# Norm statistics of the last workspace layer, queued pair by pair behind the masked steps of the layer before it

## The chip, the cores and the metric

The kernel runs on one core of a Trainium2 chip. The metric is the device time of one execution in microseconds, lower is better. The engines are TensorE (PE in the profile, with its weight loads as PEld), VectorE (DVE), ScalarE (ACT), GpSimd (POOL) and SyncE (SP), which issues the DMAs. Each engine works through a queue of its own in order, and waits on semaphores for the others.

## The reference

A stack of eight residual layers on an input of 4 sequences x 512 positions x 256 features, all float32. The last two matter here: the low-rank attention layer and the second pass of the workspace layer. Every layer normalizes its input first.

```python
def _layernorm(x, axis=-1, eps=1e-05):
    m = jnp.mean(x, axis=axis, keepdims=True)
    v = jnp.var(x, axis=axis, keepdims=True)
    return (x - m) / jnp.sqrt(v + eps)
...
    # _L1_attn_b_ref, the low-rank layer: 16 heads of 16, causal
    Q = _multilora(x, ids, Wq, Aq, Bq)
    ...
    scores = jnp.einsum('bhqd,bhkd->bhqk', Q, K) / jnp.sqrt(jnp.asarray(D_KV, x.dtype))
    causal = jnp.tril(jnp.ones((s, s), bool))
    scores = jnp.where(causal, scores, jnp.asarray(-jnp.inf, scores.dtype))
    attn = jax.nn.softmax(scores, axis=-1)
    out = jnp.einsum('bhqk,bhkd->bhqd', attn, V)
    out = out.transpose(0, 2, 1, 3).reshape(b, s, D_MODEL)
    return _multilora(out, ids, Wo, Ao, Bo)
...
    x = x + _L1_ffn_ref(_layernorm(x, axis=-1), ...)      # workspace layer, first pass
    x = x + _L1_attn_b_ref(_layernorm(x, axis=-1), ...)   # low-rank layer
    x = x + _L1_ffn_ref(_layernorm(x, axis=-1), ...)      # workspace layer, second pass
    return x
```

## The kernel before

The residual stream stays on the chip: `self.x[b]` holds sequence b as 128 partitions x 4 tiles x 256 features. A *tile* below is one of these [128, 256] pieces, numbered i. The layers run one after another. TensorE's queue is in program order; the queues of VectorE, ScalarE and GpSimd are set by a scheduler with its own estimates of time.

**The low-rank layer** (`lora_stage`, method `run`) goes through 16 units `todo`, 4 sequences x 4 groups of 4 heads. Its loop over n works on three units at once, in a pipeline. Round n has four steps m = 0 to 3:

- `maxima` of unit n + 1: TensorE makes scores (L1507) into two PSUM buffers. VectorE runs four *masked steps* on them (L256, `masked`): each adds the causal mask, and its running minimum, fetched by an accumulator read, is a row maximum with its sign turned. Step m works on 512, 384, 256 and 128 keys. Each pair of masked steps frees a PSUM buffer.
- `weights` of unit n: TensorE makes scores again (L1507), ScalarE takes the exponential (L1539, `lo_ex`), and GpSimd zeroes the upper triangle (L1540, a select).
- at m = 0, `values` of unit n - 1 (L1550 on TensorE, 32 matmuls; then ScalarE's copy to `lo_og`, L1555); at m = 1, `divided` (transposes L1563, then L1566 and L1567 on VectorE).
- at m = 3 after a sequence's last group, `output` part 0 (L1578, L1580); at m = 0 of the round after, part 1: 16 matmuls (L238) and the addition to `x` (L1591). With that the sequence's `x` is final for this layer.
- after m = 3, `lowered`: transposes (L1528) and `lo_qm` (L1530).

In some rounds `prepare` also works on the next sequence: `adapted` (matmuls L238 from `s4b`, then `lo_wvob`, L1446), `project` (matmuls L238, then L1469 on VectorE, L1473 on ScalarE, `lo_wide` L1475 and L1476 on GpSimd), `turn` (L1482, L1486). All PSUM tiles of this stage come from one tag with four buffers, used in turn:

```python
with m.psum("ps_3", two=4), pool("lora_2", 2) as l2:
    run(l2)
```

**The workspace layer** (`ws`) starts with `enter(b)` for the four sequences. `layernorm` calls `moments`: on VectorE four `bn_stats` (L178), one for each tile, and four `bn_aggr` (L179) that make mean and variance. Then the inverse root of the variance for all four tiles at once: `rpow` takes one step on VectorE (L154), Ln and Exp on ScalarE (L155, L156), and three more steps on VectorE (L157, L158, L160); L195 makes an offset. `rpow_aside` is the same with the small steps on GpSimd (L141, L144 to L147, and L192, L193 for the offset), Ln and Exp on L142 and L143; before, it serves the first pass for b = 0 and 1, and an earlier layer twice. ScalarE then writes the normalized `ws_xf` (L203).

For b = 0, 1, 2 of the second pass, the input is final long before `ws` begins, and the scheduler had put their statistics into the low-rank layer's loop: right behind the addition to `x` (L1591), in rounds n = 5, 9 and 13, among the masked steps of m = 1. The statistics of the fourth sequence have to wait for the last addition.

Of the kernel before, what the change touches and what calls it, by code (L numbers as in the profile page):

```python
# [16 lines left out]
P = 128  # L17
# [8 lines left out]
class Model:  # L26
# [142 lines left out]

        self.tc.keep_in_program_order(self.nc.scalar.preload_act_table_set("natural_log_exp_and_others"))  # L170

    def moments(self, src, aside=False):

        nc = self.nc
        st = self.small.tile([P, NI, 6], F32, name="ln_st", tag="ln_st")
        mv = self.small.tile([P, NI, 2], F32, name="ln_mv", tag="ln_mv")
        for i in range(NI):
            nc.vector.bn_stats(out=st[:, i, :], in_=src[:, i, :])  # L178
            nc.vector.bn_aggr(out=mv[:, i, :], in_=st[:, i, :])  # L179
        rstd = self.small.tile([P, NI], F32, name="ln_rstd", tag="ln_rstd")  # L180
        (self.rpow_aside if aside else self.rpow)(rstd, mv[:, :, 1], 1.0, 1e-5, self.tmps())
        return mv, rstd

    def layernorm(self, dst, src, by_scalar=False, aside=False):

        nc = self.nc
        mv, rstd = self.moments(src, aside)
        if by_scalar:
            both = by_scalar == "both"
            off = self.small.tile([P, NI], F32, name="ln_off", tag="ln_off")  # L190
            if aside:
                nc.gpsimd.tensor_tensor(off, mv[:, :, 0], rstd, op=ALU.mult)  # L192
                nc.gpsimd.tensor_scalar_mul(off, off, -1.0)  # L193
            else:
                nc.vector.scalar_tensor_tensor(off, mv[:, :, 0], -1.0, rstd, op0=ALU.mult, op1=ALU.mult)  # L195
            for i in range(NI):
                if both and i % 2:
                    nc.vector.tensor_scalar(
                        dst[:, i, :], src[:, i, :], mv[:, i, 0:1], rstd[:, i : i + 1],
                        op0=ALU.subtract, op1=ALU.mult,  # L200
                    )
                    continue
                nc.scalar.activation(  # L203
                    dst[:, i, :], src[:, i, :], AF.Identity, bias=off[:, i : i + 1], scale=rstd[:, i : i + 1]
                )
            return mv, rstd
        for i in range(NI):
            nc.vector.tensor_scalar(
                dst[:, i, :], src[:, i, :], mv[:, i, 0:1], rstd[:, i : i + 1],
                op0=ALU.subtract, op1=ALU.mult,  # L210
            )
# [41 lines left out]

    def masked(self, sc, n, nmax):

        self.nc.vector.tensor_tensor_reduce(  # L256
            out=sc[:, :n], in0=sc[:, :n], in1=self.mask[:, T - n :], scale=-1.0, scalar=3.0e38,
            op0=ALU.add, op1=ALU.min, accum_out=nmax,
        )
# [760 lines left out]
    def ws_fold(self, w, pool, once):  # L1020
# [47 lines left out]
        for h in range(4):  # L1068
            m, rows = h % 2, slice(h * 32, h * 32 + 32)
            nc.vector.tensor_tensor(w["ob"][rows], w["ob"][rows], pb[rows, m, :D], op=ALU.add)  # L1070
    def ws(self, w, order, woven={}):

        nc, S, R = self.nc, 16, P
        with self.pool("ws_1", 1) as p1, self.pool("ws_2", 2) as p2:
# [258 lines left out]

            if True:
                def enter(b):
                    mv, rstd = self.layernorm(xf[b], self.x[b], "both" if b == B - 1 else True, bool(woven) and b < 2)
                    nc.vector.tensor_tensor(ms[:, :, b], mv[:, :, 1], rstd, op=ALU.mult)
                    nc.vector.tensor_tensor(ms[:, :, b], ms[:, :, b], rstd, op=ALU.mult)
                    turned(b, int(b == 2))

                for b in range(B):
                    if b == B - 1:
                        with self.tc.high_priority(offset=2000):
                            enter(b)
                    else:
                        enter(b)
                flat = ms.rearrange("p i b -> p (i b)")
                self.rpow(
                    flat, flat, 1.0, 1e-6, [tile([P, NI * B], f"rp{k}") for k in range(2)],
                    norm.rearrange("p i (b s) -> p (i b) s", s=32),  # L1350
                )
                for rnd in range(2):
                    st = written(gathered(picked(rnd == 0)), rnd)
                    wqk, cst = folded(st)
                    vo = None
                    for n in range(B + 5):
                        if n < B:
                            attend(n, wqk, cst)
                        if n == 1:
                            vo = outputs(st)  # L1360
                        if 0 <= n - 3 < B and rnd == 0:
                            carried(n - 3)
                        if 0 <= n - 2 < B:
                            turn(n - 2)
                        if 0 <= n - 3 < B:
                            read(n - 3, vo, rnd)
                        if 0 <= n - 5 < B and rnd == 0:
                            turned(n - 5, 2 * (n > 6), True)
                        if (rnd, n) in woven:
                            next(woven[rnd, n], None)  # L1370
# [5 lines left out]
    def lora_load(self, wp, shared):  # L1376
        nc = self.nc
        st = wp.tile([P, 4], I32, name="lo_st", tag="lo_st")
        nc.sync.dma_start(out=st, in_=self.a["lo_starts"].partition_broadcast(P))
        w = {n: self.load(shared[0], f"lo_{n}") for n in ("wqk", "wvo")}  # L1380
        w |= {n: self.load(shared[1], f"lo_{n}") for n in ("aqk", "avo", "bqk")}
        w |= {n: self.load(shared[2], f"lo_{n}") for n in ("bvo", "lidx")}
        w["cos"], w["sin"] = self.load(wp, "rope16_c"), self.load(wp, "rope16_s")

        stf = wp.tile([P, 4], F32, name="lo_stf", tag="lo_stf")
        nc.vector.tensor_copy(stf, st)
        cnt = wp.tile([P, B], F32, name="lo_cnt", tag="lo_cnt")
        for b in range(B):
            le = wp.tile([P, 4], F32, name=f"lo_le{b}", tag=f"lo_le{b}")
            nc.vector.tensor_scalar(le, stf, float(b), None, op0=ALU.is_le)  # L1390
            nc.vector.tensor_reduce(cnt[:, b : b + 1], le, axis=AX.X, op=ALU.add)
        nc.gpsimd.tensor_scalar(cnt, cnt, 1.0, 0.0, op0=ALU.subtract, op1=ALU.max)
        w["lm"] = lm = wp.tile([P, B], F32, name="lo_lm", tag="lo_lm")
        nc.vector.tensor_scalar(lm, cnt, 3.0, w["lidx"], op0=ALU.min, op1=ALU.is_equal)
        return w
# [22 lines left out]
    def lora_stage(self, w, order, tiles, wpool):  # L1418
# [93 lines left out]
        def maxima(s, g, m):  # L1512

            i = NI - 1 - m
            n = (i + 1) * P
            nm = nmt[g % 2]
            scs = scored(n, slice(i * P, n), s.qk[:, 0, g, :], s.qk[:, 1, g, :n])
            with self.tc.high_priority(offset=500):
                for pair, sc in enumerate(scs):
                    for k in range(2):  # L1520
                        at = (pair * 2 + k) * 32 + ONE
                        self.masked(sc[:, k, :], n, nm[:, i, at : at + 1])

        def lowered(s, g):

# [83 lines left out]
        def run(pool):  # L1609
# [7 lines left out]
                maxima(*todo[0], m)  # L1617
            seqs[1].wqk = adapted(seqs[1], "qk")
            lowered(*todo[0])
            at = (2, 5, 6, 7, 8, 9, 10)  # L1620
            for n in range(len(todo) + 2):
                s, g = todo[n] if n < len(todo) else (None, None)
                nxt = todo[n + 1] if n + 1 < len(todo) else None
                prev = todo[n - 1] if 0 < n <= len(todo) else None
                last = todo[n - 2] if n > 1 else None
                for m in range(NI):
                    if nxt:
                        maxima(*nxt, m)
                    if prev and m == 0:
                        values(*prev)  # L1630
                    if s:
                        weights(s, g, m)
                        if s is not seqs[-1] and g * NI + m in at:
                            prepare(seqs[seqs.index(s) + 1], at.index(g * NI + m))
                    if prev and m == 1:
                        divided(*prev)
                    if prev and prev[1] == G - 1 and m == 3:
                        output(prev[0], 0)
                    if last and last[1] == G - 1 and m == 0:
                        output(last[0], 1)  # L1640
                if nxt:
                    lowered(*nxt)

        return first, run

# [7 lines left out]
def emit(tc, aps):  # L1653


    with ExitStack() as ctx:
# [49 lines left out]
        with pool("lora_1", side="right") as l1, pool("lora_w", 2) as lw, m.norms("norm_2", xn=1, xt=2):  # L1706
# [2 lines left out]
                g = first()  # L1709
                m.ws(ws, ("by", "xt", "xf"), {(1, n): g for n in (1, 2, 4, 8)})  # L1710
            with m.psum("ps_3", two=4), pool("lora_2", 2) as l2:
                run(l2)
        with m.psum("ps_4", two=2, acc=4):
            m.ws(ws, ("xf", "xt", "by"))
        m.store()


# [119 lines left out]
```

## Time and profile before

| what | value |
|---|---|
| median of 3 runs | 2172.09 us (2165.91 to 2174.39) |
| the profiled execution, its own time | 2169.45 us |
| its span, first to last instruction | 2167.7 us |
| mean granted TensorE clock | 0.969 |
| busy: PE, DVE, ACT, POOL | 92%, 59%, 35%, 27% |
| `bn_stats` (L178) in the loop | 12, mean 412 ns |
| `bn_aggr` (L179) in the loop | 12, mean 162 ns |

The profile is of one execution. "Busy" is the share of the span in which an engine ran; TensorE's includes the time in which it runs at half clock. The granted clock is a share of full speed. In timelines, the bracket behind an instruction gives how long its engine had been idle before it, and whose work ended that.

### The profile page before, as it was taken

To read this page: it belongs to the slowest core of one execution; us is meant where nothing else is said; L and a number is where in the kernel's file an instruction comes from. 1 tells how busy PE (TensorE), PEld (TensorE's weight loads), DVE (VectorE), ACT (ScalarE), POOL (GpSimd) and SP (SyncE) were. 2 spreads that over 40 slices of the span, in tenths; PEclk is the share of its full clock that TensorE was granted. 3 is DMA by queue.
4 is the path that set the end of the run, shared out by engine and by line. 5 is a ranking of instruction groups with operands and counts; after the bars stand their busy time and mean duration, and the time that the engine had idled before them with its cause. 6 is when DMAs were issued, how large, how long until landed. Compare 5 with 4: busy or idle time off the path is not lost.

```text
span 2167.7 us, 25625 instructions
## 1 busy us (share of the span) xinstructions
PE 1994.9 (92%) x9414; PEld 1066.2 (49%) x9414; DVE 1271.4 (59%) x3185; ACT 760.9 (35%) x1696; POOL 577.3 (27%) x530
## 2 busy tenths in 40 slices
PE   7999999999899999999999999987888989899886
PEld 4556555564544554544454554533355644444464
DVE  5565655756447435644754355498855766657445
ACT  2433434434323222322232233243224324334442
POOL 2433333433312112211312122175620122212100
PEclk9999999999999999999999999999799999999898
DMA  5020000000000000000000000010000000000001
GB/s 176 1 90 1 1 1 1 1 1 1 21 0 0 1 0 0 0 1 0 0 1 0 1 0 1 19 27 0 1 25 1 1 1 1 1 1 1 1 1 40
DMA packets 19837, 22.87 MB, mean 11 GB/s; under 512 B 4832, under 2 KB 17664, under 8 KB 19328
## 3 DMA queue, kind: packets, MB, share of 16 engines
q1 hardware_dynamic: 19712, 21.24, 3.0%
q8 instruction: 74, 1.21, 0.2%
q14 instruction: 51, 0.42, 0.1%
HBM read 19.14 MB, written 2.10 MB: 10 GB/s over the span
## 4 chain that ended last, share of the span: by engine, by line
PE 63%; DVE 16%; issue 11%; ACT 5%; POOL 3%; DMA 1%; SPq 0%; POOLq 0%; DVEq 0%; ACTq 0%
PE ps_two L238 26%; PE ps_acc L238 11%; PE ps_two L390 5%; PE ps_acc L429 3%; PE ps_two L1507 3%; DVE ps_two L256 3%; PE ps_two L417 2%; POOL e L687 2%; PE ps_two L1550 2%; DVE gs L888 1%; PE ps_acc L1248 1%; DVE ln_st L178 1%; PE ps_two L654 1%; ACT prob L397 1%; PE ps_st L884 1%
## 5 line engine op out<-in xcount | busy, mean ns | idle before, releaser
L687 POOL TENSOR_TENSOR e<-e 128x1024 f32<-128x1024 f32 x64 | 150.7, 2355 | 619.4 <-ACT e L679 592.2
L256 DVE CUSTOM_DVE_ANT_0 ps_two<-ps_two,mask 128x256 f32<-128x256 f32 (+3 forms) x512 | 249.6, 503 | 71.8 <-PE ps_two L390 40.8
L679 ACT ACTIVATE e<-ps_two 128x1024 f32<-128x1024 f32 x128 | 130.7, 1023 | 346.9 <-PE ps_two L238 346.7
L238 PE MATMUL ps_acc<-e,cv 128*128 128x512 f32 x512 | 234.9, 601 | 1.4 <-DVE cot L685 0.9
L402 POOL TENSOR_TENSOR prob<-prob,psum_row 128x256 f32<-128x256 f32 (+3 forms) x128 | 159.6, 1255 | 283.0 <-DVE psum_row L401 276.8
L238 PE MATMUL ps_two<-cq,ckt 128*128 128x512 f32 x512 | 230.5, 593 | 3.0 <-DVE cq L656 3.0
L397 ACT ACTIVATE prob<-ps_two,nmax 128x128 f32<-128x128 f32 (+3 forms) x256 | 132.5, 525 | 147.0 <-DVE nmax L256 137.8
L238 PEld LDWEIGHTS ps_acc<-e,cv 128*128 128x128 f32 x512 | 93.5, 190 | 138.4 <-issue 116.5
L238 PEld LDWEIGHTS ps_two<-cq,ckt 128*128 128x128 f32 x512 | 96.6, 190 | 116.9 <-issue 114.5
L238 PE MATMUL ps_two<-own_xt,s 128*128 128x512 f32 x200 | 109.6, 680 | 18.8 <-DVE prt L129 10.6
L238 PE MATMUL ps_two<-own_xt,s16a 128*128 128x512 f32 x256 | 114.9, 592 | 0.1
L238 PE MATMUL ps_two<-s16b,cot 128*128 128x256 f32 x512 | 113.1, 379 | 0.0
L1539 ACT ACTIVATE lo_ex<-ps_two 128x1024 f32<-128x1024 f32 (+3 forms) x128 | 85.2, 704 | 69.7 <-PE ps_two L1507 65.3
L390 PE MATMUL ps_two<-kvt,qx 64*128 64x256 f32 (+3 forms) x512 | 103.6, 481 | 6.1 <-ACT qx L378 2.4
L238 PEld LDWEIGHTS ps_two<-s16b,cot 128*128 128x128 f32 x512 | 97.3, 190 | 20.1 <-issue 7.7
L417 PEld LDWEIGHTS ps_two<-ident,prob 128*128 128x128 f32 x640 | 71.0, 142 | 73.4 <-issue 48.2
L417 PE MATMUL ps_two<-ident,prob 128*128 128x128 f32 x640 | 94.6, 279 | 12.9 <-ACT qx L378 4.5
L1540 POOL TENSOR_SCALAR_AFFINE_SELECT lo_ex<-lo_ex 128x256 f32<-128x256 f32 x128 | 51.7, 408 | 188.8 <-ACT lo_ex L1539 187.7
L688 DVE TENSOR_TENSOR es<-e 128x512 f32<-128x512 f32 x64 | 43.9, 686 | 95.0 <-POOL e L687 93.9
L390 PE MATMUL ps_two<-kpe,qy 64*128 64x256 f32 (+3 forms) x512 | 90.7, 431 | 0.9 <-POOL qy L324 0.9
L1507 PE MATMUL ps_two<-lo_qm,lo_t 32*128 32x128 f32 (+3 forms) x512 | 75.1, 473 | 11.1 <-ACT lo_ex L1539 4.7
L429 PE MATMUL ps_acc<-prt,kv 128*64 128x256 f32 (+3 forms) x512 | 78.8, 451 | 2.7 <-DVE prt L129 2.7
(429 smaller groups left out, 3412.6 us busy)
## 6 DMA issues: line engine op xcount, KB each, us to landing
x<-in_x SPq DMA_DIRECT2D x4, 512.0 KB, 7.5
s16b<-in_mla_wo SPq DMA_DIRECT2D x1, 2048.0 KB, 18.4
s16a<-in_cos_wq SPq DMA_DIRECT2D x1, 2048.0 KB, 8.8
s16b<-in_cos_wo SPq DMA_DIRECT2D x1, 2048.0 KB, 8.2
out_x<-x SPq DMA_DIRECT2D x4, 512.0 KB, 2.9
s16a<-in_mla_wqn SPq DMA_DIRECT2D x1, 1536.0 KB, 12.3
s<-in_mla_wqa SPq DMA_DIRECT2D x1, 1024.0 KB, 9.3
s4a<-in_mla_wkb SPq DMA_DIRECT2D x1, 512.0 KB, 6.8
```

Source lines behind the costliest of these rows:

```text
L238: self.nc.tensor.matmul(out, lhsT=l, rhs=r, start=k == 0, stop=k == n - 1)
L256: self.nc.vector.tensor_tensor_reduce(out=sc[:, :n], in0=sc[:, :n], in1=self.mask[:, T - n :], scale=-1.0, scalar=3.0e38, op0=ALU.add, op1 ...
L390: nc.tensor.matmul(sc[:, k, :n], lhsT=q[r, rows], rhs=key[r, :n], start=first, stop=not first)
L397: nc.scalar.activation(pr[:, k, :n], sc[:, k, :n], AF.Exp, bias=nm[:, k : k + 1], scale=-1.0, accum_out=sm[:, k : k + 1],)
L402: nc.gpsimd.tensor_tensor(pr[:, :, :n], pr[:, :, :n], sm.unsqueeze(2).to_broadcast([P, 2, n]), op=ALU.mult)
L417: nc.tensor.transpose(pt[:, k, keys], pr[:, k, keys], self.ident)
L429: nc.tensor.matmul(po[k * R : (k + 1) * R, j * P :], lhsT=s.kv[:, j, 0, :], rhs=prt[:, k, j, j * P :], start=j == 0, stop=j == NI - 1,)
L679: nc.scalar.activation(t.e[:, pair * 2 : pair * 2 + 2, :], sc, AF.Exp)
L687: nc.gpsimd.tensor_tensor(e2, t.e[:, 0:2, :], t.e[:, 2:4, :], op=ALU.add)
L1507: nc.tensor.matmul(scs[k // 2][:, k % 2, : keys], lhsT=left[r, rows], rhs=right[r], start=True, stop=True)
L1539: nc.scalar.activation(ex[:, hs, :], sc[:, :, :n], AF.Exp, scale=0.25)
L1540: nc.gpsimd.affine_select(out=ex[:, hs, :P], in_=ex[:, hs, :P], compare_op=ALU.is_ge, fill=0.0, base=0, pattern=[[0, 2], [1, P]], channel_ ...
```

## The change

`maxima` returns its last masked step, and `run` collects these (`ends`) and hands the second `ws` three lists of four: for each of sequences 0 to 2, the ends of m = 1, 2, 3 in the round that finishes its `x`, and of m = 0 in the next. `moments` then queues one pair of `bn_stats` and `bn_aggr` behind each of them on VectorE. The results lie in a tile of their own for each sequence (`lo_stat`) instead of rotating small buffers, and the small steps take the `rpow_aside` form, on GpSimd. In the changed kernel, the GpSimd offset steps are L198 and L199, and the statistics L185 and L186. The order behind a masked step is a place in the queue: it adds no semaphore wait.

On the queues this moves 12 `bn_stats` and 12 `bn_aggr`, takes 15 small steps off VectorE and puts 21 on GpSimd. On ScalarE the three Ln and three Exp move: for sequences 0 and 1, Ln stands ahead of the next copy to `lo_og` and Exp behind it; for sequence 2, both stand ahead of it.

```diff
-    def moments(self, src, aside=False):
+    def moments(self, src, aside=False, after=None):
...
-        st = self.small.tile([P, NI, 6], F32, name="ln_st", tag="ln_st")
-        mv = self.small.tile([P, NI, 2], F32, name="ln_mv", tag="ln_mv")
+        if after:
+            place, ends = after
+            st, mv, rstd = place[:, :, 0:6], place[:, :, 6:8], place[:, :, 8]
+        else:
...
         for i in range(NI):
-            nc.vector.bn_stats(out=st[:, i, :], in_=src[:, i, :])
-            nc.vector.bn_aggr(out=mv[:, i, :], in_=st[:, i, :])
-        rstd = self.small.tile([P, NI], F32, name="ln_rstd", tag="ln_rstd")
+            with self.tc.issue_after(ends[i].ins) if after else ExitStack():
+                nc.vector.bn_stats(out=st[:, i, :], in_=src[:, i, :])
+                nc.vector.bn_aggr(out=mv[:, i, :], in_=st[:, i, :])
         (self.rpow_aside if aside else self.rpow)(rstd, mv[:, :, 1], 1.0, 1e-5, self.tmps())
...
-                    mv, rstd = self.layernorm(xf[b], self.x[b], "both" if b == B - 1 else True, bool(woven) and b < 2)
+                    mv, rstd = self.layernorm(
+                        xf[b], self.x[b], "both" if b == B - 1 else True, b < (2 if woven else len(after)),
+                        after[b] if b < len(after) else None,
+                    )
...
+        w["stat"] = [wp.tile([P, NI, 10], F32, name=f"lo_stat{b}", tag=f"lo_stat{b}") for b in range(B - 1)]
...
                     if nxt:
-                        maxima(*nxt, m)
+                        ends.append(maxima(*nxt, m))
...
+            return [(w["stat"][n], ends[(n * G + G + 1) * NI + 1 :][:NI]) for n in range(B - 1)]
...
-                run(l2)
+                after = run(l2)
         with m.psum("ps_4", two=2, acc=4):
-            m.ws(ws, ("xf", "xt", "by"))
+            m.ws(ws, ("xf", "xt", "by"), after=after)
```

## The prediction

> **What bounds the kernel now.** I read the page first: its chain of waits says that TensorE carries the time, with VectorE behind it.
>
> ```profile
> PE 63%; DVE 16%; issue 11%; ACT 5%; POOL 3%; DMA 1%; SPq 0%; POOLq 0%; DVEq 0%; ACTq 0%
> PE ps_two L238 26%; PE ps_acc L238 11%; PE ps_two L390 5%; PE ps_acc L429 3%; PE ps_two L1507 3%; DVE ps_two L256 3%; PE ps_two L417 2%; POOL e L687 2%; PE ps_two L1550 2%; DVE gs L888 1%; PE ps_acc L1248 1%; DVE ln_st L178 1%; PE ps_two L654 1%; ACT prob L397 1%; PE ps_st L884 1%
> ```
>
> Then I asked where the twelve moved `bn_stats` (L178) run: four each at 1845.5, 1923.4 and 1999.5 us, all in the loop of the low-rank layer (about 1763 to 2038 us). I call these places batches 1, 2, 3. The timeline of batch 3 (start us, us, engine, line, in brackets the idle time before and who ended it):
>
> ```profile
> 1999.54 1.40 DVE L178 BATCH_NORM_STATS2 ln_st<-x 128x6 f32<-128x256 f32 x4
> ...
> 2001.52 0.42 PEld L1563 LDWEIGHTS ps_two<-ident,lo_og 128*128 128x128 f32 x4 [2.02 <-DVE ln_mv L179]
> ...
> 2002.75 0.21 ACT L155 ACTIVATE ln_rstd<-rp 128x4 f32<-128x4 f32 x1 [2.46 <-DVE rp L154]
> ```
>
> The four `bn_stats` stand between the first and second masked step of a group of four. Those masked steps free the PSUM buffer that TensorE needs, so TensorE sits 2.02 us. ScalarE sits 2.46 us at L155, which is queued ahead of the second exponential. In batch 1 a third wait follows:
>
> ```profile
> 1849.78 0.36 DVE L157 TENSOR_TENSOR rp<-rp,ln_rstd 128x4 f32<-128x4 f32 x1 [1.06 <-ACT ln_rstd L156]
> ...
> 1850.65 1.21 DVE L1446 TENSOR_TENSOR lo_wvob<-s,ps_two 128x1024 f32<-128x1024 f32 x1
> ...
> 1851.91 0.30 PEld L1507 LDWEIGHTS ps_two<-lo_qm,lo_t 32*128 32x128 f32 x4 [1.74 <-DVE lo_wvob L1446]
> ```
>
> VectorE waits for ScalarE before a 4-element step; behind it queues `lo_wvob`, for which TensorE waits 1.74 us.
>
> Last, an ordinary round without statistics (12.6 us long):
>
> ```profile
> 1822.90 0.59 ACT L1555 COPY lo_og<-ps_two 128x512 f32<-128x512 f32 x1 [4.11 <-PE ps_two L1550]
> 1823.42 0.14 DVE L256 DVE_READ_ACCUMULATOR2_ANT lo_nm<- 128x1 f32 x1
> 1823.62 0.31 PEld L1507 LDWEIGHTS ps_two<-lo_t 32*128 32x128 f32 x8 [0.55 <-DVE lo_nm L256]
> ...
> 1824.58 0.57 DVE L256 CUSTOM_DVE_ANT_0 ps_two<-ps_two,mask 128x384 f32<-128x384 f32 x1 [1.02 <-PE ps_two L1507]
> ...
> 1825.01 0.30 PEld L1507 LDWEIGHTS ps_two<-lo_qm,lo_t 32*128 32x128 f32 x4 [1.08 <-ACT lo_ex L1539]
> ```
>
> VectorE has gaps at fixed places: 1.02 us after the masked steps of m = 0, 0.43 before L1566, 0.75 before L1530. The copy of `lo_og` and the exponentials after it release TensorE.
>
> **The change, part by part.** On TensorE and SyncE the order of instructions stays; on ScalarE only six small steps move; on VectorE only the statistics and fifteen small steps. No DMA moves. New positions per batch: one `bn_stats` and `bn_aggr` pair behind the four masked steps of m = 1, 2, 3 of the same round, and of m = 0 of the next. Then seven small steps on GpSimd, with Ln and Exp on ScalarE.
>
> *Removed at m = 1.* The four masked steps take 2.46 us back to back (1824.58 to 1827.04). In batch 1 the first starts at 1845.05, so all end at 1847.51. One new pair follows: 0.41 for `bn_stats` plus 0.15 for `bn_aggr`, 0.55 together, to 1848.06. `lo_wvob` then waits only for TensorE's four matmuls (1.98 us, now from 1846.4), and starts at 1848.45 instead of 1850.65: 2.2 us earlier. Batch 2 the same way: masked steps from 1922.94, matmuls 1924.27 to 1926.25, `lo_wvob` at 1926.35 instead of 1927.78, 1.45 us. Batch 3 has no `lo_wvob`: masked steps 1999.06 to 2001.52, pair to 2002.07, L1566 and L1567, and m = 2 starts at 2002.7 instead of 2004.45. That is 1.75 us, and L195 (0.16) goes too: 1.9.
>
> *The other pairs.* At m = 2 in batches 1 and 2 VectorE idles afterwards (2.10 and 4.15 us before L1469): nothing. In batch 3 the steps of m = 3 follow without a gap: 0.5 lost. At m = 3 the gap is 2.76 us before L1469 (batch 1) or 0.75 before L1530 (ordinary rounds): nothing. At m = 0 of the next round it is 3.84 us or 1.02: nothing. Without this cover each pair would cost 0.55.
>
> *The small steps.* GpSimd's rows from the first use of this layer: 0.20 us each, 0.29 from start to start (L147, L192, L193), some 2.5 us a batch with the wait for ScalarE. Behind them GpSimd queues the selects of the next exponentials, whose readers come a round later, and `lo_wide`, needed more than 3 us later: nothing. The results are needed at 2038.7 us (`ws_xf`).
>
> *The added wait.* The new Ln (L142) stands on ScalarE ahead of the copy of `lo_og`, and waits for GpSimd (L141), which waits for the last `bn_aggr`. In batch 3 the Exp stands there too. By the ordinary round: the last accumulator read starts at 1823.42, `bn_stats` to 1823.83, `bn_aggr` to 1824.03, L141 to 1824.3, Ln and Exp to 1824.75. So `lo_og` is copied about 1.8 us late and the first exponential runs about 1.2 us late; TensorE's weights wait for exactly that ([1.08 <-ACT lo_ex L1539]). In batches 1 and 2 sixteen matmuls and transposes (1868.0 to 1871.7) lie before the next use of these buffers: hidden, with 1 us over. Batch 3 has none: I take 1.1 us. Bounds: 0.7 if that round starts at half clock, as it does in the trace (masked steps and L1550 then end together), and 1.8 if the whole delay of the copy counts.
>
> *Sum.* 2.2 + 1.45 + 1.9 - 0.5 - 1.1 = 3.95, say 4.0 us. The profiled execution took 2169.45 us (span 2167.7 and 1.75 around it): 2165.5. It lies 2.6 us below the median 2172.09, so on that 2168.0.
>
> **Rivals.**
>
> *The clock gives more.* In windows of 10 us (columns: length; busy and count of PE, PEld, DVE, ACT, POOL; granted clock; DMA; GB/s) the clock falls just behind batches 2 and 3:
>
> ```profile
> 1920.00:1930.00 10.00, 8.06 (x47) 4.33 (x47) 7.55 (x27) 2.16 (x6) 1.22 (x3) 1.00 0.00 0
> 1930.00:1940.00 10.00, 8.44 (x31) 4.06 (x30) 3.67 (x17) 2.09 (x5) 2.95 (x6) 0.71 0.01 2
> 2000.00:2010.00 10.00, 7.59 (x46) 4.49 (x48) 7.87 (x37) 3.07 (x8) 2.40 (x6) 0.63 0.01 2
> ```
>
> The same projections take 9.2 us in batch 1 (1853.72 to 1862.94) and 12.9 in batch 2 (1930.59 to 1943.53): 3.7 us. In batch 3, L1528, L1507 and L1550 take 1.11, 2.09 and 3.15 against 0.66, 1.14 and 2.36: 2.2 us. If shorter waits keep the clock up, 5.9 us come on top: 2162.1. Against: batch 1 had the same waits without a dip, ordinary rounds show dips (granted clock 0.84 in 1890 to 1900), and earlier starts shift every later dip. Chance 0.14. The Trainium skill, "TensorE: Matmul & The Clock Gate", section "What's actually happening", says that the clock halves after an idle window of about 3.4 us and that the windows run freely. By that rule alone no wait here is long enough, and this rival would give nothing; the trace does not agree, since the clock fell after single waits of 2.02 us at most.
>
> *Slower: Ln ahead of `lo_og`.* If the cover in batches 1 and 2 fails too, the whole delay of the copy counts three times, 5.4 us, and m = 2 and m = 0 add 0.55 each in those batches. Against 2.2 + 1.45 + 1.9 - 0.5 = 5.05 that is 2.5 us more than before: 2174.6. It decides from about 1.7 us a batch. For: the wait crosses three engines. Against: 3 us of TensorE work before the buffers' next use. Chance 0.12.
>
> *It changes nothing.* The masked steps end earlier but TensorE meets the next wait (0.55 for a masked step, 0.47 for an exponential) at the old time: 2172. Against: these waits hang on the same chain, which moves as a whole. Chance 0.11.
>
> **How the numbers follow.** The forecast (gain 2 to 6 us) has 0.60; 0.03 is left for what I do not see. Likeliest time 2168.0. The range runs from the clock rival with 2 us for the spread of runs, 2160, to the slower rival, 2174.5; the runs before alone span 8.5 us. 0.5% is 10.9 us, about what a measurement of this kernel can tell from no change. All named cases lie inside it; the clock rival reaches its edge (2161.2), so I give 0.08 to faster, 0.04 to slower, 0.88 between.
>
> **What would show it.** Right: the 2.02 us waits of TensorE at L1563 and the s4b matmuls shrink to about 0.55; ScalarE's 2.46 us before L155 goes; `lo_wvob` starts about 4.5 us after the `x` addition in batches 1 and 2 (now 6.7 and 6.0); after batch 3, `lo_og` waits about 1.8 us longer. Wrong: TensorE waits for `lo_og` or `lo_ex` by more than 1.7 us in batches 1 and 2; VectorE's pairs push L1469 or L1530; or rows outside the loop move.

## The result and the profile after

The changed kernel takes 2165.38 us (median of 13 runs, 2160.53 to 2168.2); the kernel before took 2172.18 in 13 runs beside them. The ratio is 0.9966, 95% interval 0.9958 to 0.9975: 6.8 us faster, 5.4 to 9.1. The forecast was 2168.0, and its range holds the result. The profiled execution of the changed kernel took 2168.2 us (span 2166.5, granted clock 0.967) and is the slowest of its 13 runs; the profile of before lies 2.7 us under its median. So the two profiles are compared by rounds and rows, not by their spans.

The chain of waits of the changed kernel, from its page, by engine:

```profile
PE 64%; DVE 16%; issue 11%; ACT 5%; POOL 3%; DMA 1%; SPq 0%; POOLq 0%; DVEq 0%; ACTq 0%
```

The shares are those of before but for one per cent of TensorE: over the whole span the change is small, and the rows have to show it. The timeline of batch 1 (start us, us, engine, line; in brackets the idle time before and who ended it). Lines have moved: L256 is L262, L1446 is L1458, L1507 is L1519.

```profile
1846.53 1.22 DVE L1604 TENSOR_TENSOR x<-x,ps_two 128x1024 f32<-128x1024 f32 x1 [3.92 <-PE ps_two L244]
...
1848.99 0.30 PEld L244 LDWEIGHTS ps_two<-s4b,lo_amvo 128*128 128x128 f32 x2 [0.89 <-DVE lo_nm L262]
...
1849.97 0.42 DVE L185 BATCH_NORM_STATS2 lo_stat<-x 128x6 f32<-128x256 f32 x1
...
1850.43 0.18 DVE L186 BATCH_NORM_AGGREGATE lo_stat<-lo_stat 128x2 f32<-128x6 f32 x1
...
1851.02 1.22 DVE L1458 TENSOR_TENSOR lo_wvob<-s,ps_two 128x1024 f32<-128x1024 f32 x1 [0.41 <-PE ps_two L244]
...
1852.29 0.30 PEld L1519 LDWEIGHTS ps_two<-lo_qm,lo_t 32*128 32x128 f32 x4 [0.64 <-DVE lo_wvob L1458]
```

TensorE waits 0.89 us for its PSUM buffer instead of 2.02. VectorE no longer waits for ScalarE: `lo_wvob` waits only for TensorE's matmuls (0.41) and starts 4.49 us after the addition to `x` (1846.53), where it took 6.73. TensorE's wait for it is 0.64 instead of 1.74.

Batch 3 and the round behind it:

```profile
1995.63 0.42 PEld L1576 LDWEIGHTS ps_two<-ident,lo_og 128*128 128x128 f32 x4 [0.90 <-DVE lo_nm L262]
...
2004.58 2.41 PE L1563 MATMUL ps_two<-lo_ex,lo_v 128*32 128x512 f32 x32
...
2008.49 0.21 ACT L142 ACTIVATE lo_stat<-rp 128x4 f32<-128x4 f32 x1 [7.44 <-POOL rp L141]
...
2008.73 0.21 ACT L143 ACTIVATE lo_stat<-lo_stat 128x4 f32<-128x4 f32 x1
...
2008.84 0.57 ACT L1568 COPY lo_og<-ps_two 128x512 f32<-128x512 f32 x1
...
2009.46 0.30 PEld L1519 LDWEIGHTS ps_two<-lo_t 32*128 32x128 f32 x4 [1.38 <-ACT lo_og L1568]
```

The values end at 2006.99 (2004.58 plus 2.41), and the copy to `lo_og` starts at 2008.84: behind Ln and Exp, as forecast, and TensorE waits 1.38 us for it.

Below, "round n" is measured from the start of its `values` matmuls (L1550 before, L1563 after) to those of the next round; the last column runs from the start of round n = 5 to that of n = 16. All are worked out from the start times in the traces, in us:

| kernel | n = 5 (batch 1) | n = 9 (batch 2) | n = 13 (batch 3) | n = 14 | n = 5 to 15 |
|---|---|---|---|---|---|
| before | 27.86 | 30.57 | 20.33 | 12.70 | 195.75 |
| changed | 25.64 | 25.38 | 18.54 | 15.07 | 188.73 |

So the loop gives 7.0 us in these two profiles: 2.22 in batch 1, 5.19 in batch 2, 1.79 in batch 3, less 2.37 given back in round n = 14; the other rounds add 0.2. Behind the loop, from the start of round n = 16 to the end, this execution of the changed kernel is longer than that of before, 138.3 us against 135.2, at a granted clock of 0.91 against 0.93. Two things are open after this: batch 2, for which the sum had 1.45, and how much of all this is the clock. The last windows of 10 us that bear on it, of the changed kernel (columns: length; busy and count of PE, PEld, DVE, ACT, POOL; granted clock; DMA; GB/s):

```profile
1929.00:1939.00 10.00, 8.92 (x55) 5.19 (x57) 5.53 (x19) 2.35 (x5) 3.50 (x6) 1.00 0.00 1
...
2014.00:2024.00 10.00, 9.31 (x80) 5.04 (x82) 4.46 (x19) 2.42 (x5) 1.65 (x5) 0.61 0.01 2
```

Behind batch 2 the granted clock is now 1.00, where it was 0.71. Behind batch 3 the stretch of low clock is still there, but later: 0.61.

### The profile page after: what moved, and what is told of

Its sections match the earlier page's. It is cut to its first block, busy times and chain, and to the rows that moved or that the text cites. A ratio compares the mean times of both kernels' runs of the same rounds, so it can differ in the third digit from the quotient of the medians.

```text
span 2166.5 us, 25623 instructions
## 1 busy us (share of the span) xinstructions
PE 1998.5 (92%) x9414; PEld 1066.8 (49%) x9414; DVE 1270.4 (59%) x3170; ACT 759.8 (35%) x1696; POOL 580.7 (27%) x551
## 4 chain that ended last, share of the span: by engine, by line
PE 64%; DVE 16%; issue 11%; ACT 5%; POOL 3%; DMA 1%; SPq 0%; POOLq 0%; DVEq 0%; ACTq 0%
PE ps_two L244 27%; PE ps_acc L244 11%; PE ps_two L396 5%; PE ps_two L1519 4%; PE ps_acc L435 3%; DVE ps_two L262 3%; PE ps_two L423 2%; POOL e L693 2%; PE ps_two L1563 2%; DVE gs L894 1%; PE ps_acc L1255 1%; PE ps_two L660 1%; DVE ln_st L185 1%; ACT prob L403 1%; PE ps_st L890 1%
## 5 line engine op out<-in xcount | busy, mean ns | idle before, releaser
L262 DVE CUSTOM_DVE_ANT_0 ps_two<-ps_two,mask 128x256 f32<-128x256 f32 (+3 forms) x512 | 249.7, 503 | 73.4 <-PE ps_two L396 41.2
L403 ACT ACTIVATE prob<-ps_two,nmax 128x128 f32<-128x128 f32 (+3 forms) x256 | 132.3, 525 | 147.8 <-DVE nmax L262 138.6
L1519 PE MATMUL ps_two<-lo_qm,lo_t 32*128 32x128 f32 (+3 forms) x512 | 75.7, 475 | 9.6 <-ACT lo_ex L1552 4.3
```

Of the source, the lines that this page charges most:

```text
L262: return self.nc.vector.tensor_tensor_reduce(out=sc[:, :n], in0=sc[:, :n], in1=self.mask[:, T - n :], scale=-1.0, scalar=3.0e38, op0=ALU.a ...
L403: nc.scalar.activation(pr[:, k, :n], sc[:, k, :n], AF.Exp, bias=nm[:, k : k + 1], scale=-1.0, accum_out=sm[:, k : k + 1],)
L1519: nc.tensor.matmul(scs[k // 2][:, k % 2, : keys], lhsT=left[r, rows], rhs=right[r], start=True, stop=True)
```

## The experiments

Two theories were held against each other. W: the waits give the 4.0 us of the sum, and the rest comes from the granted clock. S: the waits give all of it, and a term of the sum was mis-sized. To part them, the 161 runs of the 13 kernels below that have a clock on record were fitted with one slope of time on mean granted clock and one level for each kernel: the slope is -1.41 us (standard error 0.09) for each 0.001 of clock. "At equal clock" below is the difference of levels, with its standard error. It takes a loss of clock to cost the same wherever it falls in the kernel, which no run shows.

| kernel | median us (runs) | ratio to before, 95% | mean clock | at equal clock, against before | n = 5 to 15 |
|---|---|---|---|---|---|
| before | 2170.97, 2171.38, 2171.35 (57 in three sets) | 1 | 0.9682 | 0 | 195.75 |
| changed, again | 2162.82 (6) | 0.9963 [0.9949, 0.9978] | 0.9703 (with the first 13) | -4.0 +- 0.45 | 188.72 |
| engine alone | 2164.25 (12) | 0.9972 [0.9962, 0.9983] | 0.9703 | -2.95 +- 0.5 | 191.13 |
| late Ln and Exp | 2160.25 (6) | 0.9949 [0.9933, 0.9965] | 0.9717 | -5.1 +- 0.75 | 187.22 |
| no statistics | 2162.25 (6) | 0.9957 [0.9944, 0.9971] | 0.9712 | -4.6 +- 0.7 | 183.53 |
| sequences 0 and 1 | 2166.78 (7) | 0.9976 [0.9965, 0.9987] | 0.9686 | -3.8 +- 0.6 | 188.49 |
| sequence 2 | 2170.37 (11) | 0.9992 [0.9983, 1.0001] | 0.9692 | +0.6 +- 0.5 | 194.92 |
| steps on VectorE | 2164.27 (5) | 0.9962 [0.9949, 0.9974] | 0.9706 | -3.4 +- 0.8 | 188.53 |
| other gaps | 2161.43 (5) | 0.9944 [0.9932, 0.9957] | 0.9716 | -5.8 +- 0.8 | 185.14 |

**The changed kernel again.** No edit.

> The changed kernel once more, for rows and clocks of both kernels on one chip. Theory W (waits): the removed waits give 4.0 us as summed in the prediction (2.2 + 1.45 + 1.9 - 0.5 - 1.1), and the other 2 to 3 us of the 6.8 measured come from the granted clock, so runs of both kernels with the same granted clock differ by about 4 us. Rival S (sizes): the waits give all 6.8 us because a term of the sum was mis-sized (the 1.1 us for Ln and Exp ahead of the copy to lo_og is the most doubtful), so runs at the same clock differ by about 6.8 us. Both expect 5.5 to 8 us below the kernel before in the median.

At equal clock the changed kernel, with all its 19 runs, lies 4.0 us (standard error 0.45) below the kernel before; 6.8 would be six standard errors off. That speaks for W. The traces say the same without the fit: in rounds n = 5 to 15 TensorE was at half clock for 23.9 us before and for 17.1 us after (mean clock 0.939 and 0.955). If its work takes twice as long there, the clock accounts for 3.4 of the 7.0 us and 3.6 are left for the waits; that is an estimate. The profile of this second execution repeats the rounds of the first to 0.02 us (25.64, 25.38, 18.54, 15.09), and the 138.3 us behind the loop too. Both executions took longer than the median of their sets; what the others do behind the loop is not on record.

**The engine alone.** Small steps on GpSimd, the pairs left in the old place.

```diff
-            with self.tc.issue_after(ends[i].ins) if after else ExitStack():
+            with ExitStack():
```

> The small steps by GpSimd alone: the statistics stay where the kernel before had them, four in a row among the masked steps of m = 1. Theory W: TensorE's waits of 2.02 us stay, and only what the small steps cost goes: in batch 1 VectorE's wait for ScalarE (1.06) and some 0.5 for the steps, in batches 2 and 3 up to 0.5 each; Ln and Exp still stand somewhere in ScalarE's queue. So 1 to 2 us below the kernel before, about 2170.5 to 2171. Rival (engine): the small steps off VectorE are the main thing and the placement is not; then it equals the changed kernel, 6 to 7 us below the kernel before.

By its median this kernel is where the rival had it, 6.7 us below the kernel before: the clock rises as much as with the whole change. At equal clock it stands at 2.95 us, 1.05 short of the changed kernel (standard error 0.6), and the rows say where. Its batch 2, in the timeline:

```profile
1926.26 1.22 DVE L1604 TENSOR_TENSOR x<-x,ps_two 128x1024 f32<-128x1024 f32 x1 [4.03 <-PE ps_two L244]
...
1929.85 0.30 PEld L244 LDWEIGHTS ps_two<-s4b,lo_amvo 128*128 128x128 f32 x2 [2.02 <-DVE lo_stat L186]
...
1931.87 1.22 DVE L1458 TENSOR_TENSOR lo_wvob<-s,ps_two 128x1024 f32<-128x1024 f32 x1 [0.84 <-PE ps_two L244]
...
1933.15 0.30 PEld L1519 LDWEIGHTS ps_two<-lo_qm,lo_t 32*128 32x128 f32 x4 [0.64 <-DVE lo_wvob L1458]
```

The wait of 2.02 us is still there, but `lo_wvob` no longer waits for ScalarE. It starts 5.61 us after the addition. And the clock behind it, in windows of 10 us:

```profile
1924.00:1934.00 10.00, 8.35 (x49) 4.56 (x49) 6.87 (x22) 2.57 (x6) 2.69 (x11) 1.00 0.00 0
1934.00:1944.00 10.00, 8.79 (x50) 5.39 (x52) 5.07 (x21) 2.62 (x6) 2.94 (x6) 1.00 0.01 2
```

1.00, with the 2.02 us wait kept. Round n = 9 lasts 26.50 us, 4.07 less than before. So the low clock behind batch 2 did not hang on that wait alone. The placement itself is worth 26.50 - 25.38 = 1.12 us in batch 2, all of it in `lo_wvob` (5.61 - 4.49). In batch 1 the engine alone brings nothing here: round n = 5 lasts 28.24 us, `lo_wvob` starts 7.09 us after the addition, and the low clock lies in this round (0.94). In batch 3, 19.48 against 18.54 is no comparison at one clock (0.79 and 0.91). By the times the engine is the larger part of the gain, 2.95 of 4.0 us, where W had 1 to 2. That the placement adds to it is shown by batches 1 and 2, not by the whole time, where 1.05 is under two standard errors.

**Ln and Exp later.** For all three sequences they stand on ScalarE behind the exponentials of m = 0, so the copy to `lo_og` is not behind them.

```diff
-        (self.rpow_aside if aside else self.rpow)(rstd, mv[:, :, 1], 1.0, 1e-5, self.tmps())
+        with self.tc.issue_after(act.ins) if after else ExitStack():
+            (self.rpow_aside if aside else self.rpow)(rstd, mv[:, :, 1], 1.0, 1e-5, self.tmps())
...
-            return [(w["stat"][n], ends[(n * G + G + 1) * NI + 1 :][:NI]) for n in range(B - 1)]
+            return [(w["stat"][n], ends[(n * G + G + 1) * NI + 1 :][:NI], acts[(n * G + 6) * NI]) for n in range(B - 1)]
```

> As the changed kernel, but Ln and Exp of all three sequences are queued on ScalarE behind the exponentials of m = 0, so that the copy to lo_og is not behind them. Theory W: in round n = 14 the copy to lo_og starts when the values are done, and the round is 1.1 us (0.7 to 1.8) shorter than in the changed kernel at the same clock; batches 1 and 2 unchanged, since 16 matmuls hid the copy. So about 1.1 us below the changed kernel, 2164.3. Rival S: the late copy costs nothing, and the kernel equals the changed one within 0.3 us.

Round n = 14 of this kernel:

```profile
2010.16 0.58 ACT L1570 COPY lo_og<-ps_two 128x512 f32<-128x512 f32 x1 [7.44 <-PE ps_two L1565]
...
2012.27 0.30 PEld L1520 LDWEIGHTS ps_two<-lo_qm,lo_t 32*128 32x128 f32 x4 [1.08 <-ACT lo_ex L1553]
...
2013.01 0.21 ACT L142 ACTIVATE lo_stat<-rp 128x4 f32<-128x4 f32 x1
```

The copy waits only for the values, the round lasts 13.02 us instead of 15.07, and the rounds n = 5 and 9 are the same to 0.01 us: in batches 1 and 2 Ln ahead of the copy cost nothing, as the prediction had it. At equal clock the gain over the changed kernel is 5.1 - 4.0 = 1.1 us, as W expected, with a standard error of 0.7; the medians, 2160.25 against 2162.82, have overlapping ranges. The two rounds, however, did not have the same clock: 0.88 here, 0.73 in the changed kernel. A round with the late copy at nearly the clock of this one stands in the changed kernel with 16 transposes more (below):

```profile
2008.14 0.30 PEld L1519 LDWEIGHTS ps_two<-lo_t 32*128 32x128 f32 x4 [0.60 <-ACT lo_og L1569]
```

It lasts 13.25 us at 0.89. So in a round that begins at half clock, as these two do, the late copy costs 0.2 us and not 1.1; most of the 2.05 us is low clock, which takes less of the round here. Rival S is not excluded for such a round.

**No statistics.** Statistics and small steps of the three sequences left out.

```diff
+        if after:
+            return mv, rstd
...
+        for t in w["stat"]:
+            nc.gpsimd.memset(t, 1.0)
```

> Leaves out the statistics and the small steps of the three sequences altogether (the tile that should hold them is set to 1.0). It gives the ceiling of what any placement can bring. Theory W: against the changed kernel it saves the late copy (1.1) and the pair at m = 2 of batch 3 (0.5) and the three pairs at m = 1 (0.55 each, 1.65): 3 us below it, about 2162.4, and 7 us below the kernel before at the same clock. Rival S: if the waits already gave 6.8, the most that is left is the 1.65 us of the pairs at m = 1, about 2163.8.

Rounds n = 5 and 9 last 25.63 and 25.38, to 0.01 us as in the changed kernel: there the eight pairs and the small steps are free, the pairs at m = 1 too, which W had priced at 0.55 each. In batch 3 0.64 us is left (17.90 against 18.54), and 3.4 in round n = 14 (11.64), which here has a granted clock of 0.99 instead of 0.73: most of that is the clock. The stretch n = 5 to 15 is 5.2 us shorter than in the changed kernel; the whole time hardly shows it (2162.25 against 2162.82). At equal clock it lies 0.6 us (standard error 0.7) below the changed kernel, where W had 3, and 4.6 below before, where W had 7: W missed here. The likely reason is that the pairs at m = 1 and the late copy cost less than it had.

**One part of the batches each.**

```diff
-            return [(w["stat"][n], ends[(n * G + G + 1) * NI + 1 :][:NI]) for n in range(B - 1)]
+            return {n: (w["stat"][n], ends[(n * G + G + 1) * NI + 1 :][:NI]) for n in range(B - 1) if n < 2}
```

The other kernel has `if n == 2`.

> The change for sequences 0 and 1 alone; the third keeps its statistics and small steps where the kernel before had them. Theory W (the waits as summed, the clock beside them): rounds n = 5 and 9 last 25.6 and 25.4 us as in the changed kernel, batch 3 and round n = 14 as in the kernel before; 2.2 + 1.45 = 3.65 us below the kernel before at the same granted clock. If the granted clock follows the waits removed, its mean over the runs lies between the 0.968 of the kernel before and the 0.9705 of the changed one, nearer to the changed one (two of the three batches), and the median comes to about 2165. Rival T (the third batch makes the clock, since the longest half-clock stretch, 10.2 us, lies on it): the mean clock stays at 0.968 and the median at about 2167.5.

> The change for sequence 2 alone; sequences 0 and 1 keep their statistics and small steps where the kernel before had them. Theory W: 1.9 - 0.5 - 1.1 = 0.3 us below the kernel before at the same granted clock, the round of batch 3 at 18.5 us and the next at 13.8 at full clock; mean clock near 0.969, median about 2170. Rival T: the clock gain sits here, the mean clock is 0.9705 and the median about 2167.

At equal clock the gain sits in sequences 0 and 1: 3.8 us (3.65 expected), and the third gives nothing that can be told (0.6 slower, standard error 0.5; 0.3 faster expected). With sequence 2 alone changed, round n = 9 lasts 30.60 us and round n = 5 28.24; with 0 and 1 changed, 25.38 and 25.64. The mean clock rises by 0.0010 with sequence 2 and by 0.0004 with 0 and 1, against 0.0021 with all three: neither part holds the clock gain alone. Rival T, which gave it to the third batch, falls with the median of 2170.37. But W missed too: with 0 and 1 changed it expected most of the clock gain and 2165, and 2166.78 came. The loop of that kernel is 7.3 us shorter than before, the median only 4.6; in its profile the part behind the loop takes 138.6 us instead of 135.2, as in the changed kernel. Why these kernels lose clock there is open.

**Small steps on VectorE.** Pairs placed as in the change.

```diff
-                        xf[b], self.x[b], "both" if b == B - 1 else True, b < (2 if woven else len(after)),
+                        xf[b], self.x[b], "both" if b == B - 1 else True, bool(woven) and b < 2,
```

> The pairs placed as in the changed kernel, the small steps back on VectorE, behind the last pair; there VectorE waits for Ln and Exp of ScalarE. Theory W: the pairs give 1.12 us in each of batches 1 and 2 and 0.94 in batch 3 on top of what the engine alone gives (the rounds of the kernel with the engine alone against the changed one: 26.50 against 25.38, 19.48 against 18.54), and the wait of VectorE for Exp in m = 0 is some 1 to 1.5 us a batch: hidden in batches 1 and 2 by the 3.84 us gap there, open in round n = 14, where it delays the masked steps of m = 1 by up to 1 us. So 0 to 1 us above the changed kernel at the same clock. Rival (engine): the engine is the main thing, and this kernel falls back to within 1 us of the kernel before.

Its round n = 14, VectorE:

```profile
2011.89 0.17 DVE L154 TENSOR_SCALAR rp<-lo_stat 128x4 f32<-128x4 f32 x1
2012.57 0.17 DVE L157 TENSOR_TENSOR rp<-rp,lo_stat 128x4 f32<-128x4 f32 x1 [0.52 <-ACT lo_stat L156]
...
2013.53 0.57 DVE L262 CUSTOM_DVE_ANT_0 ps_two<-ps_two,mask 128x384 f32<-128x384 f32 x1 [0.18 <-PE ps_two L1519]
```

VectorE waits 0.52 us for Exp, and the masked steps still wait for TensorE behind it. Rounds n = 5 and 9 are unchanged, the level is 0.6 above the changed kernel's (standard error 0.8), inside what W expected. The rival, within 1 us of before, falls. Once the pairs stand in the gaps, no difference between the engines can be told.

**Other gaps, a better version.** Late Ln and Exp, and the third sequence's pairs and small steps further back.

```diff
+            at = [[(n * G + G + 1) * NI + k for k in (1, 2, 3, 4)] + [(n * G + 6) * NI] for n in range(2)]
+            at.append([55, 56, 59, 59, 63])
+            return [(w["stat"][n], [ends[k] for k in ks[:NI]], acts[ks[NI]]) for n, ks in enumerate(at)]
```

> A version that may beat the changed one: Ln and Exp of sequences 0 and 1 behind the exponentials of m = 0, and the third sequence's pairs moved to where VectorE has gaps (m = 3 of round n = 13, m = 0 and twice m = 3 of round n = 14), its small steps behind the last exponential of the loop. Theory W: the 0.64 us by which round n = 13 of the changed kernel (18.54) is longer than without statistics (17.90) goes, and the late copy to lo_og in round n = 14 goes (1.1 us); the two pairs at m = 3 of n = 14 push L1543 by 0.55 at most. So 1.2 to 1.7 us below the changed kernel at the same clock, the median about 2161 to 2163. Rival: late pairs move into the front of the workspace layer, which then starts later; no gain over the changed kernel.

Rounds n = 13 and 14 last 16.49 and 11.73 us, 5.4 less than in the changed kernel together, at clocks of 1.00 and 0.98 instead of 0.91 and 0.73, so that most of it is again the clock. The level is 1.8 below (standard error 0.8; W expected 1.2 to 1.7). The ratio to before is 0.9944, but its interval [0.9932, 0.9957] touches the changed kernel's [0.9949, 0.9978]: faster than before, and against the changed kernel likely, not shown.

**Does the clock's part depend on where the rounds fall?** Both kernels with more transposes ahead of the batches, to move all that follows.

```diff
-            for i in range(NI):
-                nc.tensor.transpose(pt[:, i * P : (i + 1) * P], nmt[g % 2][:, i, :], self.ident)
+            for k in range(5 if s is seqs[0] and g == 1 else 1):
+                for i in range(NI):
+                    nc.tensor.transpose(pt[:, i * P : (i + 1) * P], nmt[g % 2][:, i, :], self.ident)
```

The second pair makes those of `lo_og` 8 times in the same way.

> The kernel before with 16 transposes more on TensorE (the four of lo_nm of unit 1 made five times over), in a round ahead of all three batches: everything behind comes later by some 2.4 us (16 by 0.15 to 0.16, the pitch of L1528's four in 0.66), 0.7 of the 3.41 us by which the trace's clock steps are spaced. Theory W (it is the waits that lower the clock of the kernel before): its mean clock stays at 0.968, the median at 2171.2 + 2.4 = 2173.6. Rival P (the clock's part of the gain is only where the stretches happen to fall): the mean clock moves away from 0.968 by 0.0015 or more, up to the changed kernel's 0.970, and the median comes to 2171 or less.

> The changed kernel with the same 16 transposes. Theory W: its mean clock stays near 0.970, 0.002 above the kernel before with the same delay, and the median is 6.8 us (5.5 to 8) below it. Rival P: the gap in clock between the two goes or turns over, and the medians differ by the waits alone, 4.0 us, or less.

> The kernel before with 28 transposes more (the four of lo_og of unit 1 made eight times over), in a round ahead of all three batches: about 4.1 us later (28 by 0.147), one clock step and 0.2 of a second. Theory W: mean clock 0.968, median 2175.3. Rival P: the mean clock moves by 0.0015 or more.

> The changed kernel with the same 28 transposes. Theory W: mean clock near 0.970, the median 6.8 us (5.5 to 8) below the kernel before with the same delay. Rival P: the gap in clock goes or turns over, and the medians differ by about 4.0 us or less.

| delay | before: median, clock | changed: median, clock | difference |
|---|---|---|---|
| none | 2171.35 (23), 0.9682 | 2165.38 (13) and 2162.82 (6), 0.9703 | 6.0 and 8.5 us |
| 16 transposes | 2170.69 (11), 0.9687 | 2162.98 (5), 0.9712 | 7.7 us |
| 28 transposes | 2173.05 (12), 0.9680 | 2165.89 (5), 0.9722 | 7.2 us |

The medians differ as W expected, and the gap in clock stays in each pair (0.0021, 0.0025, 0.0042). At equal clock the pairs differ by 5.0 and 2.4 us, with standard errors of 0.9. W's medians for the kernel before, 2173.6 and 2175.3, were 3 and 2 us too high.

But the delays did not move what they were to move. In the kernel before, measured from the first scores of this layer, the 16 transposes delay round n = 1 by 1.8 us (27.31 against 25.53) and round n = 5 by only 0.1 (96.17 against 96.09). The 28 delay round n = 5 by 4.5, but rounds n = 9 and 13 by 3.3, nearly one unit of 3.41 us. By the times of the clock steps in the traces, round n = 9 starts 0.89 us into such a unit in the kernel before, 0.97 and 0.76 with the delays, and 0.73 in the kernel with sequence 2 alone: always at about the same place. So these runs do not show what the kernel before would do elsewhere, and do not by themselves rule out Rival P. The windows behind batch 2 of the kernel before with 16 transposes:

```profile
1934.00:1944.00 10.00, 8.44 (x31) 4.18 (x32) 3.77 (x18) 2.18 (x5) 2.94 (x6) 0.71 0.00 1
```

The same 0.71. In all four profiles that have batch 2 as before (the kernel before with and without the two delays, and the one with sequence 2 alone) round n = 9 lasts 30.53 to 30.60 us; in all nine with its pairs moved or left out, 25.37 or 25.38. These nine start it at 0.25 to 1.92 us of the unit, the changed kernel itself at 0.87. That settles batch 2: at the same place of the unit the kernel before has the low clock and the changed kernel has not, and elsewhere the changed ones do not have it either.

In batch 1 the place does count. Round n = 5 of before lasts 27.86 us at full clock where it starts 1.5 or 1.6 us into the unit, and 28.24 to 28.27 us at 0.94 where it starts at 2.6 (28 transposes, sequence 2 alone). With the pairs moved or left out it lasts 25.63 or 25.64 at either place.

## Why the prediction was right, point by point

**Batch 1, 2.2 us: right.** Round n = 5 went from 27.86 to 25.64, 2.22; `lo_wvob` starts 4.49 us after the addition, 4.5 forecast.

**Batch 2, 1.45 us (1.43 by its own two times): right for the waits; here the sum failed, by the term that it put at nothing, the clock.** `lo_wvob` starts 4.49 us after the addition here too, but the round became 5.19 us shorter. The rest, 3.74, is what the rival "the clock gives more" had for this place: 3.7, the projections at 12.9 us instead of 9.2. The prediction saw it, gave it 0.14, and argued against it that earlier starts only shift the low clock, and that batch 1 had the same waits without a dip. The runs say otherwise: the dip went in each of the nine profiles in which batch 2 was changed, also where the round starts at the same place of the clock's unit; and batch 1 of before has a dip too where it starts elsewhere in the unit.

**Batch 3, 1.9 - 0.5: right.** The masked steps of m = 2 start 4.61 us after the addition (1997.77 - 1993.16) instead of 6.52, 1.9 earlier; those of m = 3 (2000.09) are 1.5 earlier, so the pair at m = 2 cost 0.4. The round is 1.79 us shorter, but not at the same clock (0.91 against 0.79), so that figure does not confirm the sum.

**Round n = 14, 1.1 us lost: the mechanism is there, the size is not confirmed.** TensorE waits 1.38 us for `lo_og`, whose copy starts 1.85 us after the values (1.8 forecast). But the rounds say less than 1.1 where they can be compared: 13.25 and 12.91 us in the changed kernels with delays, at clocks of 0.89 and 0.90, against 13.02 without the late copy (0.88) and 12.70 before (0.90). These begin at half clock, the case for which the prediction had 0.7, and lose 0.2. Where the round begins at full clock it lasts 15.07 and 15.09, but there the low clock of batch 3 falls into it (0.73), and what the wait alone costs cannot be told. The late copy does not bring that low clock by itself: the two kernels with delays have the copy and not the stretch. So the rival's second part, 2.2 us in batch 3, came only in part: rounds n = 13 and 14 together last 33.0 us before, 33.6 in both profiles of the changed kernel, and 31.2 and 31.4 in those with delays.

**TensorE's waits of 2.02: right in direction.** They fell to 0.89 and 0.90, not 0.55.

**Covers and rivals.** The pairs elsewhere and the small steps on GpSimd cost nothing in batches 1 and 2 (the rounds without statistics are the same length); the slower rival, Ln ahead of `lo_og` exposed three times, fell with that. "It changes nothing" fell with round n = 5. The prediction's sign "rows outside the loop move" did appear, behind the loop (138.3 us against 135.2), with the clock.

**The total.** The sum, 4.0, agrees with the fit at equal clock, 4.0 +- 0.45, and with the 3.6 us estimated from the rounds; in the pairs with delays the fit gives 5.0 and 2.4. Since the term for round n = 14 is not confirmed, agreement to a tenth is partly luck. The 2.6 us between forecast and median go with the clock: 0.0021 higher, times 1.41 us for 0.001, is 3.0 us. The low clock that went behind batch 2 is one source of it. The rest is not placed, and low clock elsewhere, in round n = 14 and behind the loop, takes some of it back in the profiled executions.

## What to carry to other kernels

Where one engine frees the buffers of another, put small work for later behind the last instruction that frees one, and look in the round itself for the gap that takes it: here the eight pairs of batches 1 and 2 cost nothing at all. Steps that wait for another engine do harm by what is queued behind them, so price that first, in the new place too. Add up the waits that go as one sum, and the low-clock stretches that follow them as a second one, and give the second its own term wherever the same stretch stands behind the same place. To test whether such a stretch hangs on a place in time, check in the trace that the delay arrives there: here it was gone after a few rounds.

## What the runs showed of the hardware

The clock steps in units of 3.41 us, and one unit follows how busy TensorE was in the unit before. Over the 14 profiles, of the units at full clock: with TensorE at matmuls (their ends are modelled) for less than 1.4 us, 126 of 126 were followed by half clock; with 1.4 to 1.7 us, 78 of 95; with 1.7 to 2.85 us, 110 of 959; above that, 0 of 6848. (The start and the end of each trace are left out.) Of the 314 stretches of half clock begun, only 6 follow a unit without any work on TensorE. The longest idle time in the unit ahead was 1.7 us in the median. So several short waits in one unit are enough, and no single wait need be long. The Trainium skill, "TensorE: Matmul & The Clock Gate", section "What's actually happening", has the same free-running unit of 3413 ns and puts the half clock behind an idle one; the traces agree on the unit and not on the idleness.

The stretches behind batches 2 and 3 belong to the unsettled middle: TensorE was busy for 1.9 to 2.8 us in the units ahead of them, most of it with score matmuls of 32 rows (L1519). What tips them is open: in batch 2 of the kernel with the engine alone it was enough that the small steps left VectorE, in a round that starts at the same place of the unit (0.72 us) as with sequence 2 alone (0.73), where the low clock stayed.
